# First steps' cached keys gathered and turned, rotation tables and key mask made within layer 0; first half of layer 0's base product as seven block products

## The chip, the cores and the metric

The kernel runs on one core of a Trainium2 chip. Its time is the device time of one execution in microseconds (us); the figure compared is the median of several runs. The engines of the core are named as in the profile: PE (TensorE, matmuls), DVE (VectorE), ACT (ScalarE), POOL (GpSimd), SP (SyncE, which only issues DMAs). Each takes its instructions from a queue of its own, in order.

## What is computed

Four layers follow each other on 8 x 128 tokens of width 512, each of the form x = x + ffn(cond(x)). Two matter here. Layer 0 ends with a mixture of eight low-rank experts over a base product, and layer 2's first part is attention with a paged key and value cache. In the reference's words, cut:

```python
def _L0_ffn_ref(x, base_W, router_W, lora_A, lora_B):
    base = jnp.einsum('bsd,od->bso', x, base_W)
    probs = softmax(einsum('bsd,ed->bse', x, router_W))      # top 2 of 8, renormalised: w_dense
    mid = jnp.einsum('bsd,edr->bser', x, lora_A) * w_dense[..., None]
    return base + jnp.einsum('bser,erd->bsd', mid, lora_B) * 2.0

def _L2_cond_ref(x, Wq, Wk, Wv, Wo, q_norm_w, k_norm_w, k_cache, v_cache, block_table, cache_seqlens):
    q, k, v = projections of x                               # 32 query heads, 8 key heads of 128
    q = _rope(_rmsnorm(q, q_norm_w), pos); k = _rope(_rmsnorm(k, k_norm_w), pos)
    kc = k_cache[block_table]; vc = v_cache[block_table]     # 512 cached tokens of each sequence
    scores = q @ [kc, k] / sqrt(128), -1e30 where the cached key is past cache_seqlens
    return softmax(scores) @ [vc, v] @ Wo.T
```

x here is the output of layer 0's first part, a gated unit with a hidden width of 1376, for the experts, and layer 1's output for the attention.

## The kernel before

All data are fp32; x stays in SBUF as four chunks of 128 features by 1024 tokens. The work is one long program for one core; the tile framework gives buffers and semaphores, and may reorder instructions on an engine unless they are marked (`kept`, in the change also `held`: `keep_in_program_order`). `tc.issue_after(i)` holds instructions back in the order until after i.

**Layer 0, first part.** The hidden units are made in 11 chunks (`gates`, `gates_by_seven`). The second product (`Down`, L598) takes each pair of token quarters (g = 0, 1) and each pair of output chunks (k = 0, 1) by Strassen's scheme: seven block products in place of eight, with sums of weight blocks (`down_weights`, L532, on POOL) and of hidden blocks (`h_sums`, L545, on DVE). `begin`, `go_on` and `out` issue the products, the intermediate reads (L625, L626, L628) and the final sums into `y0` (L640, L642). `transposed(Ad)` uses the buffers tagged `Ad` and `Bg`, which are free afterwards.

**Layer 0, experts** (`experts`, L221). Per half of the tokens: `mids` makes the router logits and low-rank values (L53, copied at L241), `route` the weights (L249 to L277, a chain of small DVE operations with one exponential on ACT), `mix` turns them (L288, L290), and `outs` adds for each of four output chunks the base product, four matmuls of 128x512 over `base0`, and the low-rank product, one matmul, in one bank, and adds the bank to x (L305). The first half's `mids0` and `route0` run among the last `Down` products; `mix0(0)`, `outs0(0)`, and the whole second half follow after the layer's pools have been closed and the attention's pools opened in the same memory. Layer 1 (`adapt`, `mids1`, ..., `outs1`) follows with small products.

**Attention** (`attention`, L807). At its opening DVE makes the mask `hide` (L826 to L834) and POOL the four rotation tables (L844: cosines and sines times the norm weights). The work is 32 steps: 8 key heads x 4 pairs of sequences. Per step n:
- `gather(n, "k")` and `gather(n, "v")`: eight indirect DMAs each, issued by POOL (L928);
- `turn_cached` (L1120): DVE transposes the keys in 32x32 blocks (L1125), SP writes them to DRAM (L1134) and loads them back fully turned into `kT` (L1130);
- `project`: q, k, v by seven products (`seven`, L971; matmuls L985, DVE reads L998, L1000, L1034);
- `squares`, `rotate` (POOL multiplies L1084, DVE L1089), `roots` (for steps 0 and 1 on POOL, L1107 and L1108), `rotated` (L1101), `normed` (L1118): norm and rotation;
- `turn` or, for steps 0 and 1, `turn_at_once` (PE transposes, L1159);
- `weigh`: scores and exponentials (L1179, L1183); `added`, `summed`, `inverted`: the row sums on DVE (L1199, L1209, L1210) and their inverse `R`, by way of DRAM; `mix`: values (L1231); `divided` (L1241); `leave`: output product (L985) with additions to `y2`.

Steps 0 and 1 are woven into the end of layers 0 and 1 by `begin`, `begun` and `first` (L1289 to L1330); `run` (L1332) does the rest. In `first`, `rest()` is called from within step 1's projection; in it POOL clears `y2` (`memset`, L1322). In `run`, POOL then has step 1's rotation (L1084), `roots(1)`, and `gather(2, "k")`; within step 0's part of the loop it has `gather(1, "v")`.

Of the kernel before, what the change touches and what calls it, by code (L numbers as in the profile page):

```python
# [10 lines left out]
F32 = mybir.dt.float32  # L11
I32 = mybir.dt.int32
AF = mybir.ActivationFunctionType
ALU = mybir.AluOpType
# [33 lines left out]
def forward(ctx: ExitStack, tc: tile.TileContext, a: dict, out: bass.AP):  # L48
# [16 lines left out]
    rp = c1.enter_context(tc.tile_pool(name="rp", bufs=1, side="right"))  # L65

    x = xpool.tile([P, DC, NT], F32, tag="x", name="x")

    c0 = ExitStack()
    w0 = c0.enter_context(tc.tile_pool(name="w0", bufs=1))  # L70
# [103 lines left out]


    mask1 = const.tile([P, NB], F32, tag="mask1", name="mask1")
    bias3 = const.tile([P, NB, 8], F32, tag="bias3", name="bias3")
    kvrow = {
        what: const.tile([P, NQ, NB * 4], I32, tag="kvrow_" + what, name="kvrow_" + what) for what in "vk"
# [143 lines left out]
    with c0:  # L323
# [256 lines left out]
        def ranks_to_ranks(wb1T):  # L580
# [2 lines left out]
                mm(ps, wb1T[:, c, :], wmr1[:, c, :], c == 0, c == DC - 1)  # L583
            act.copy(w11, ps)

        tdm = w0.tile([P, NT // 4], F32, tag="tdm", name="tdm")

        def lora_down(AdT):
# [55 lines left out]
        def psp_bank(shape, name):  # L644
            return psp.tile(shape, F32, tag="mm", name=name)

        HB_ = []
        downs = [Down(0, k) for k in range(2)]

# [8 lines left out]
            lora_down(AT)  # L658

        h_sums(0, ypool.tile([P, 3, NH, NT // 4], F32, tag="y", name="hs_0"), meanwhile)  # L660
        for d in downs:
            d.go_on()
        h_sums(1, st.tile([P, 3, NH, NT // 4], F32, tag="hs", name="hs_1", bufs=1), HB_.append)
        y0 = ypool.tile([P, DC, NT], F32, tag="y", name="y0")
        for d in downs:
            d.out()
# [1 line left out]
        downs = [Down(1, k) for k in range(2)]  # L668
        downs[0].begin()
        downs[0].go_on()  # L670
        mids0, route0, mix0, outs0 = experts("l0", wmr0, "probs", 2.0, None, wB0, base0, y0, add_to_x)[:4]
        mids0(0, psp_bank)
        route0(0)
        downs[1].begin()
        downs[1].go_on()
        for d in downs:
            d.out()

# [3 lines left out]
    with psa:  # L682
        c2 = psa.enter_context(ExitStack())
        ps_ = psa.enter_context(tc.tile_pool(name="psa", bufs=2, space=PSUM, reuse_waits="tile"))
        sums = nc.dram_tensor("sums", (HQ * NB // REP, REP * P), F32, kind="Internal").ap()

        def small_bank(shape, name):
            return ps_.tile(shape, F32, tag="av", name=name)

        def large_bank(shape, name):  # L690
            return ps_.tile(shape, F32, tag="st", name=name, bufs=3)


        att = attention(tc, a, x, ident, lens, kvrow, part, ww, wop, ypool, sums, rot, eps, ps_, c2, chunks, mm)

        l1 = att.scratch([P, DC * P + NT], "l1")
        wa1 = l1[:, 0 : DC * P].rearrange("p (c r) -> p c r", c=DC)
        sp.dma_start(wa1, chunks(a["wa1"]))
        t1 = l1[:, DC * P : DC * P + NT]

        def adapt(g):
            tok = slice(g * 512, (g + 1) * 512)
            ps = small_bank([P, 512], f"t1_{g}")
            for c in range(DC):
                mm(ps, wa1[:, c, :], x[:, c, tok], c == 0, c == DC - 1)
            return block_masked(t1[:, tok], ps, mask1, g)

        mids1, route1, mix1, outs1 = experts(
            "l1", None, None, 16.0, br.unsqueeze(1).to_broadcast([P, NB, 8]), wB1, None, None, add_to_x,
            mid_of=lambda tok: [(t1[:, tok], w11)],  # L710
        )[:4]

        mix0(0, large_bank)
        outs0(0, (0, 1), large_bank)
        mids0(1, small_bank)
        route0(1)
        outs0(0, (2, 3), large_bank)
        mix0(1, small_bank)
        outs0(1, (0, 1), large_bank)
        adapted = adapt(0)  # L720
        outs0(1, (2, 3), large_bank)
        mids1(0, small_bank)
        route1(0)
        att.begin()
        att.begun(adapted)
        adapt(1)
        mix1(0, small_bank)
        outs1(0, range(DC), large_bank)
        mids1(1, small_bank)
        route1(1)  # L730
        att.first(lambda: mix1(1, small_bank), lambda *o: outs1(1, o, large_bank))
        kept = nc.dram_tensor("kept_x", (P, DC, NT), F32, kind="Internal").ap()
        c1.close()
        cl = ExitStack()
        late = cl.enter_context(tc.tile_pool(name="late", bufs=1, side="right"))

        def bank(tag, shape, name):
            return ps_.tile(shape, F32, tag=tag, name=name, bufs=2 if tag == "av" else 3)

        def room(tag, shape, name):  # L740

            return (ypool if tag == "y" else wop).tile(shape, F32, tag=tag, name=name)

        def end_of(in_order):
            return ending(
                tc, a, out, x, ident, bias3, experts, late,
                lambda shape, name: ww.tile(shape, F32, tag="q7", name=name),
                lambda shape, name: ww.tile(shape, F32, tag="qs", name=name), room, chunks, mm, in_order,
            )

        y2, end = att.run(late, end_of, bank, lambda: sp.dma_start(kept, x))
        c2.close()
        c3 = ExitStack()
        w3 = c3.enter_context(tc.tile_pool(name="w3", bufs=1, reuse_waits="tile"))
        ex["sm"] = c3.enter_context(tc.tile_pool(name="sm3", bufs=2, side="right", reuse_waits="tile"))
        end.open3(w3, ex["sm"])
        end.layer2(y2, bank, do=range(NB - 2, NB))
# [46 lines left out]
            end.layer3(bank)  # L804


def attention(tc, a, x, ident, lens, kvrow, part, ww, wop, ypool, sums, rot, eps, psa, c2, chunks, mm):  # L807

# [7 lines left out]
    NP = NB // 2  # L818

    ap = c2.enter_context(tc.tile_pool(name="ap", bufs=1))  # L820
    trig, straight, crossed = rot


    kpos = ap.tile([P, 4], F32, tag="kpos", name="kpos")
    for c in range(4):
        dve.tensor_scalar(kpos[:, c : c + 1], part, float(c * P), None, ALU.add)  # L826
    hide = ap.tile([P, NB, 4], F32, tag="hide", name="hide")
    dve.tensor_tensor(
        hide,
        kpos.unsqueeze(1).to_broadcast([P, NB, 4]),  # L830
        lens.unsqueeze(2).to_broadcast([P, NB, 4]),
        ALU.is_ge,
    )
    dve.tensor_scalar(hide, hide, NEG, None, ALU.mult)  # L834


    tabs = {}
    for m in ("k", "q"):
        ws = ap.tile([P, NB, HD], F32, tag="ts" + m, name="ts" + m)
        wx = ap.tile([P, NB, HD], F32, tag="tx" + m, name="tx" + m)  # L840
        for dst, w, tr in ((ws, straight[m], "cos"), (wx, crossed[m], "sin")):
            for i in range(2):
                h = slice(i * 64, (i + 1) * 64)
                pool.tensor_tensor(  # L844
                    dst[:, :, h], w[:, h].unsqueeze(1).to_broadcast([P, NB, 64]), trig[tr], ALU.mult
                )
        tabs[m] = (ws, wx)


    half = ap.tile([P, 2, REP + 1], F32, tag="half", name="half")  # L850
    pool.memset(half, -0.5)
# [1 line left out]
    for k in range(4):  # L853
# [7 lines left out]

    steps = [(qd, p) for qd in range(NQ) for p in range(NP)]
    S = {n: {} for n in range(len(steps))}
    turned, turned_new = (
        nc.dram_tensor("turned_" + name, (len(steps), 4, 32, 4, m, 32), F32, kind="Internal").ap()
        for name, m in (("cached", 8), ("new", 2 * REP + 2))
    )
    W, WO = {}, {}


# [43 lines left out]
    def every(ops):  # L914
        for _ in ops:
            pass
# [203 lines left out]
    def turn_cached(n):  # L1120

        s = S[n]
        t = wk.tile([P, 4, 8, 32], F32, tag="kt", name=f"kt_{n}", bufs=1)
        for j in range(2):
            kept(dve.transpose(  # L1125
                t[:, :, 4 * j : 4 * j + 4, :], s["kc"][j].rearrange("p c (b d) -> p b c d", b=4)
            ))
        s["kT"] = wk.tile([P, 4, 8, 32], F32, tag="kT", name=f"kT_{n}")
        written(turned[n], t)
        return lambda: kept(sp.dma_start(s["kT"], turned[n].rearrange("b i a m d -> (b i) a m d")))  # L1130

    def written(dst, t, by=(sp,)):
# [148 lines left out]

    Y = []

    def scratch(shape, name):
        return wk.tile(shape, F32, tag="pT", name=name)

    late = []

    def begin():  # L1289
        weights(0)  # L1290
        out_weights(0)
        gather(0, "k")
        gather(0, "v")
        every(W[0].factors())

    def begun(behind):

        with tc.issue_after(behind.ins):
            turn_cached(0)()
        gather(1, "k")  # L1300

    def first(mixed, outs_):

# [1 line left out]
        running.append(True)  # L1305
        later = tokens(1, "pT")
        project(0, {
            "u2": lambda: turn_cached(1)(),
            "c22": lambda: every(later),
            "c11": lambda: (squares(0, "k", 0, (0,)), squares(0, "q", 0, (0, 1))),  # L1310
            "c12": lambda: squares(0, "q", 0, (2, 3)),
# [4 lines left out]
        def rest():  # L1316
            squares(0, "q", 1, range(REP))
            squares(0, "k", 1, (0,))
            roots(0)
            y2 = ypool.tile([P, NB, D], F32, tag="y", name="y2")  # L1320
            Y.append(y2)
            kept(pool.memset(y2, 0.0))  # L1322
            keys_terms()
            outs_(0)
            outs_(1)
            rotated(0)
            normed(0)
            outs_(2, 3)
# [3 lines left out]
    def run(pool_, end_of, bank, keep):  # L1332
# [16 lines left out]
        for n, (qd, p) in enumerate(steps):  # L1349
# [40 lines left out]
            summed(n, 0)  # L1390
            if n == 0:
                next(sums_of)
                gather(1, "v")
            every(sums_of)
            if n == 0:
                turn_at_once(1)
# [943 lines left out]
```

## Time and profile before

| | |
|---|---|
| median of 3 runs | 1488.01 us (1486.08 to 1489.38) |
| the profiled execution | 1486.79 us, of it the profiled span 1485.0 us |
| busy: PE, DVE, ACT, POOL | 1471.3, 1063.7, 563.6, 856.4 us |
| TensorE's granted clock | 0.999 |
| PE waits between 210 and 280 us | none listed |
| attention's steps 0 and 1 begin | near 291 us (first `q_one`) |

The profile comes from one execution. It lists every instruction with its start and duration, and for an engine's idle time what released it, inferred from the semaphores. A timeline row reads: start in us from the span's start, us of the group, engine, line and operation, output and inputs by tile name, shapes, how many instructions; in brackets the idle time before it and its releaser. fp32 matmuls show as two records each. "issue" stands for idle time in which the engine waited for nothing that the profile shows.

### The profile page before, as it was taken

The numbers are of one execution on the slowest core, as the hardware profiler recorded it, in microseconds if no ns is written. First come the engines' busy times: TensorE is split into PE (matmuls) and PEld (weight loads), VectorE is DVE, ScalarE is ACT, GpSimd is POOL, SyncE is SP. The second block draws the span as 40 slices with busy tenths as digits, with TensorE's granted clock in tenths as the row PEclk, the third lists the DMA queues.
The fourth block names the chain that finished last, engine by engine and source line by source line (L and its number), as shares of the span: only waits on it lengthen the run. The fifth ranks groups of instructions, "written<-read, shape, count | busy, mean of one in ns | idle before, by whom it ended". The sixth has DMA issues, their size and how long they took to land.

```text
span 1485.0 us, 18055 instructions
## 1 busy us (share of the span) xinstructions
PE 1471.3 (99%) x5571; PEld 934.6 (63%) x5571; DVE 1063.7 (72%) x2121; ACT 563.6 (38%) x1426; POOL 856.4 (58%) x876
## 2 busy tenths in 40 slices
PE   9999999999999999999999999999999999999998
PEld 7888786455556555555655555555555555558886
DVE  4665425478878787787888778787878878855475
ACT  1111110044445544444554454554445455431110
POOL 2241105477767777776777777777777777622310
PEclk9999999999999999999999999999999999999999
DMA  7411001214555544453454455345445534433001
GB/s 242 121 44 32 23 1 62 88 41 126 183 158 148 153 131 128 150 181 117 135 157 129 128 167 172 107 135 164 129 124 165 170 107 137 120 107 98 1 8 52
DMA packets 155993, 172.29 MB, mean 116 GB/s; under 512 B 52784, under 2 KB 126256, under 8 KB 155760
## 3 DMA queue, kind: packets, MB, share of 16 engines
q1 hardware_dynamic: 137712, 134.04, 30.6%
q0 software_dynamic: 17056, 36.49, 7.8%
q8 instruction: 47, 0.77, 0.2%
q10 hardware_dynamic: 1120, 0.52, 0.1%
q14 instruction: 58, 0.48, 0.1%
HBM read 129.95 MB, written 40.76 MB: 115 GB/s over the span
## 4 chain that ended last, share of the span: by engine, by line
PE 94%; DVE 3%; DMA 1%; issue 1%; ACT 0%; SPq 0%; DVEq 0%; ACTq 0%
PE st L1179 18%; PE av L1231 17%; PE g L367 9%; PE q_six L985 8%; PE q_one L985 6%; PE q_five L985 6%; PE wo_two L985 5%; PE dn L367 5%; PE wo_one L985 4%; PE wo_six L985 3%; PE eo_l L53 3%; PE h L1767 2%; PE z L1767 2%; PE o L1767 1%; PE midp_l L53 1%; PE gu L367 1%
## 5 line engine op out<-in xcount | busy, mean ns | idle before, releaser
L928 POOL DMA_INDIRECT kn<-in_k_cache,kvrow_k x256 | 272.1, 1063 | 77.2 <-issue 70.3
L928 POOL DMA_INDIRECT vals<-in_v_cache,kvrow_v x256 | 271.4, 1060 | 73.6 <-issue 59.6
L1231 PE MATMUL av<-pT,vals 128*128 128x512 f32 x640 | 290.8, 592 | 0.2 <-DVE oT L1241 0.2
L1183 ACT ACTIVATE pT<-st,hide 128x512 f32<-128x512 f32 x256 | 175.9, 687 | 191.9 <-PE st L1179 164.3
L1179 PE MATMUL st<-qT,kT 128*128 128x512 f32 x512 | 236.2, 594 | 0.3
L1231 PEld LDWEIGHTS av<-pT,vals 128*128 128x128 f32 x640 | 121.4, 190 | 152.7 <-issue 149.5
L1084 POOL TENSOR_TENSOR vq<-q,txq 128x256 f32<-128x256 f32 x128 | 121.1, 976 | 132.9 <-ACT sqq L1058 93.4
L1179 PEld LDWEIGHTS st<-qT,kT 128*128 128x128 f32 x512 | 96.3, 190 | 110.2 <-issue 105.0
L1199 DVE TENSOR_TENSOR part<-pT 128x512 f32<-128x512 f32 x128 | 88.3, 691 | 77.6 <-ACT pT L1183 64.5
L985 PE MATMUL q_one<-q,x 128*128 128x384 f32 x256 | 93.0, 486 | 0.0
L1058 ACT ACTIVATE sqq<-q 128x128 f32<-128x128 f32 x252 | 78.2, 310 | 10.6 <-DVE q L1034 4.0
L985 PEld LDWEIGHTS q_one<-q,x 128*128 128x128 f32 x256 | 48.5, 190 | 39.8 <-issue 14.1
L985 PE MATMUL q_six<-q_s,xs_all 128*128 128x384 f32 x192 | 69.8, 486 | 0.0
L1039 ACT COPY q<-q_one 128x256 f32<-128x256 f32 x32 | 11.9, 372 | 151.8 <-PE q_one L985 133.5
L985 PE MATMUL wo_one<-o,oT 128*128 128x256 f32 x256 | 65.8, 379 | 0.7 <-DVE oT L1241 0.7
L1179 PE MATMUL st<-qT,kTn 128*128 128x512 f32 x128 | 65.4, 592 | 0.0
L985 PE MATMUL wo_two<-o_s,os 128*128 128x256 f32 x256 | 60.6, 380 | 0.3 <-DVE os L944 0.3
L1183 ACT ACTIVATE pT<-st,rs 128x512 f32<-128x512 f32 x64 | 44.0, 687 | 38.6 <-PE av L1231 13.4
L985 PEld LDWEIGHTS wo_one<-o,oT 128*128 128x128 f32 x256 | 48.6, 190 | 14.2 <-DVE oT L1241 0.8
L436 POOL TENSOR_TENSOR ws<-wu 128x256 f32<-128x256 f32 (+1 forms) x9 | 6.4, 712 | 86.5 <-DMA wu<-in_WuT 86.5
L1215 ACT COPY rows<-rows 32x32 f32<-32x32 f32 x96 | 20.7, 216 | 93.0 <-DVE rows L1210 89.7
L367 PE MATMUL g<-xs,ws 128*128 128x256 f32 (+1 forms) x240 | 55.1, 379 | 0.0
(466 smaller groups left out, 2832.5 us busy)
## 6 DMA issues: line engine op xcount, KB each, us to landing
turned_new<-qkt SPq DMA_DIRECT2D x120, 160.0 KB
turned_cached<-kt SPq DMA_DIRECT2D x128, 128.0 KB
kT<-turned_cached SPq DMA_DIRECT2D x32, 512.0 KB
R<-sums SPq DMA_DIRECT2D x32, 512.0 KB
qT<-turned_new SPq DMA_DIRECT2D x30, 512.0 KB
q<-in_WqT SPq DMA_DIRECT2D x8, 1024.0 KB
o<-in_WoT SPq DMA_DIRECT2D x8, 1024.0 KB
kn<-in_k_cache,kvrow_k POOLq DMA_INDIRECT x256
```

The source lines that it names most:

```text
L53: pe.matmul(o, lhsT, rhs, start=start, stop=stop)
L367: pe.matmul(o, lhsT, rhs, start=start, stop=stop, skip_group_check=True)
L928: kept(pool.indirect_dma_start(out=d[:, c, :], out_offset=None, in_=kc if what == "k" else vc, in_offset=bass.IndirectOffsetOnAxis(ap=kvro ...
L985: kept(pe.matmul(o, l[:, c, :], r[:, c, :], start=start and c == 0, stop=c == 1, skip_group_check=True))
L1058: kept(act.activation(sq, S[n][m][:, j, i, :], AF.Square, accum_out=S[n]["ssq"][:, j, col : col + 1]))
L1084: kept(pool.tensor_tensor(to, t[:, b, :, hi : hi + 64], wx[:, b, lo : lo + 64].unsqueeze(2).to_broadcast(list(to.shape)), ALU.mult,))
L1179: kept(pe.matmul(ps, s["kT"][:, c, 4 * j : 4 * j + 4, :] if c < 4 else s["kn"][:, j], s["qT"][:, :, REP * j : REP * (j + 1), :].rearrange( ...
L1183: kept(act.activation(pT[:, c, :, :].rearrange("p i t -> p (i t)"), ps, AF.Exp, **(dict(bias=hide[:, b, c : c + 1]) if c < 4 else dict(bia ...
L1199: kept(dve.tensor_tensor(o, l, r, ALU.add))
L1215: kept(act.copy(rows[0:32, g, :], rows[32 * g : 32 * g + 32, 0, :]))
L1231: kept(pe.matmul(ps, v[:, c, :], pT[:, c, :, :].rearrange("p i t -> p (i t)"), start=c == 0, stop=c == NC - 1, skip_group_check=True,))
L1767: return pe.matmul(o, lhsT, rhs, start=start, stop=stop, skip_group_check=True)
```

## The change

It has five parts.
1. Within layer 0, behind POOL's weight sums, POOL gathers the cached keys of step 0, later of step 1 (buffer `Ad`), DVE transposes them (buffer `Bg`), and SP writes them to DRAM. In the attention `turn_cached(0)` and `turn_cached(1)` are gone; `cached(0)` and `cached(1)` only load `kT`.
2. The four rotation tables are made by DVE instead of POOL, between the first `Down` of the second half and `route0(0)`, and written to DRAM; the attention loads them (four DMAs of 512 KB on SP).
3. The mask `hide` is made in layer 0, ahead of the last `Down`'s `out()`.
4. The base product of the first token half is taken by seven block products (`Based`), for two pairs of output chunks: 28 matmuls of 128x256 in place of 16 of 128x512; the low-rank product becomes 8 of 128x256 in place of 4 of 128x512. `base_sums` (DVE, in layer 0) and `block_sums` (DVE, after the pools have changed) make the sums. Each k has three intermediate DVE reads and seven DVE additions to x.
5. Gathers move: `gather(0, "v")` waits for layer 1's first adapter product, the sums of step 0's projection weights wait for `finished`, and `gather(1, "v")` stands in `rest()`, right after the `memset` of `y2`, instead of in step 0's part of the loop.

On the engines the order in the compiled program is as written: POOL has `memset(y2)`, eight `vals` gathers of step 1, then step 1's rotation, `roots(1)`, `gather(2, "k")`. PE has step 1's transposes (`turned_1`) at the same place as before, ahead of the last five value products of step 0. DVE interleaves the second half's routing with the block products' reads.

```diff
+        def gather_keys(n):
+            first_keys[n] = t = w0.tile([P, 2, 4, HD], F32, tag="Ad", name=f"kn_{n}")
+            for i in range(8):
+                kept(pool.indirect_dma_start(out=t[:, i // 4, i % 4, :], ...
+        def turn_keys(n):
+            t = w0.tile([P, 4, 8, 32], F32, tag="Bg", name=f"kt_{n}")
+            for j in range(2):
+                kept(dve.transpose(t[:, :, 4 * j : 4 * j + 4, :], ...
+            for q in range(4):
+                kept(sp.dma_start(turned_cached[n][:, :, q]..., t[32 * q : 32 * q + 32]))
+        def rotation_tables():
+            for m, of in enumerate("kq"):
+                for i, (w, tr) in enumerate(((straight[of], "cos"), (crossed[of], "sin"))):
+                    t = w0.tile([P, NB, HD], F32, tag=("Ad", "Bg")[i], name=f"table_{of}{i}")
+                    for l in range(2):
+                        kept(dve.tensor_tensor(t[:, :, h_], w[:, h_]..., trig[tr], ALU.mult))
+                    kept(sp.dma_start(tables_kept[m, i], t.rearrange("p b d -> p (b d)")))
+                yield
...
-        for d in downs:
-            d.go_on()
+        gather_keys(0)
+        downs[0].go_on()
+        turn_keys(0)
+        gather_keys(1)
+        downs[1].go_on()
         h_sums(1, ...)
+        turn_keys(1)
...
         downs[0].begin()
         downs[0].go_on()
+        tabling = rotation_tables()
+        next(tabling)
+        next(tabling)
...
         downs[1].go_on()
+        A0 = base_sums()
+        hidden()
         for d in downs:
             d.out()
...
+            def go_on(self):
+                self.into(odd[:, 1], s1, t1, True)
+                self.into(odd[:, 0], s2, t2)
+                held(dve.tensor_tensor(u, odd[:, 0], p1, ALU.add))
+                held(dve.tensor_tensor(p1, odd[:, 1], p1, ALU.add))
+                self.into(even[:, 1], s3, t3)
+                held(dve.tensor_tensor(p1, even[:, 1], p1, ALU.add))
+                self.into(odd[:, 1], s4, b22)
+                self.into(even[:, 0], a12, b21)
+                self.into(even[:, 1], a22, t4)
...
+        based = [Based(0, k).begin() for k in range(2)]
+        block_sums(0, [yt0[:, n] for n in range(4)])
         mix0(0, large_bank)
-        outs0(0, (0, 1), large_bank)
         mids0(1, small_bank)
+        for b in based:
+            b.go_on()
+            finished = b.finish()
         route0(1)
-        outs0(0, (2, 3), large_bank)
         mix0(1, small_bank)
...
     def begin():
         weights(0)
         out_weights(0)
-        gather(0, "k")
-        gather(0, "v")
-        every(W[0].factors())
+        tabled()
-    def begun(behind):
+    def begun(behind, done):
         with tc.issue_after(behind.ins):
-            turn_cached(0)()
-        gather(1, "k")
+            gather(0, "v")
+        with tc.issue_after(done.ins):
+            every(W[0].factors())
+        for n in range(2):
+            cached(n)()
...
         project(0, {
-            "u2": lambda: turn_cached(1)(),
...
             kept(pool.memset(y2, 0.0))
+            gather(1, "v")
             keys_terms()
...
             if n == 0:
                 next(sums_of)
-                gather(1, "v")
```

## The prediction

> **What bounds the kernel now.** I read the page first, busy time and chain, then who TensorE waited for, then the timelines of the engines from 165 us to 350 us, where all edits lie.
>
> ```profile
> PE 1471.3 (99%) x5571; PEld 934.6 (63%) x5571; DVE 1063.7 (72%) x2121; ACT 563.6 (38%) x1426; POOL 856.4 (58%) x876
> ...
> PE 94%; DVE 3%; DMA 1%; issue 1%; ACT 0%; SPq 0%; DVEq 0%; ACTq 0%
> ```
>
> TensorE is busy 99% of the span and makes up 94% of the chain; its granted clock is 0.999. So only two things change the time: matmul passes taken from TensorE, and stalls put into it or taken out. The list of TensorE's waits between 210 and 420 us is short:
>
> ```profile
> PE q_six L985 <- issue: 1.6, 1, 1.6
> PE midp_l L53 <- DVE l L309: 0.8, 1, 0.8
> ```
>
> No earlier stall stands there that earlier keys, tables or mask could remove. The price of a matmul comes from the chain in order of time (start, us, what; each fp32 matmul shows as two records):
>
> ```profile
> 251.06 8.58 PE eo_l L53 x20
> ...
> 347.96 0.86 PE wo_one L985 x4
> ```
>
> Ten 128x512 matmuls take 8.58 us, 0.86 each; two 128x256 take 0.86, 0.43 each. Half the width costs half, and a product can be cut without loss.
>
> **The block product.** Removed: 16 base matmuls of 512 columns, 16 x 0.86 = 13.75 us. Added: 2 x 7 x 2 = 28 of 256 columns, 28 x 0.43 = 12.03. The low-rank part stays even (4 x 0.86 against 8 x 0.43). TensorE gains **1.7 us**, no more.
> Against it stand VectorE's answers. Each block product needs two reads of one bank (0.42 us each, row of the `du_dn`/`dp_dn` adds) before TensorE may add to that bank again. In layer 0's own block product five matmuls, 2.15 us, cover them. In the new class only two (0.86 us), or four for the first half, because the order list puts the second half's first product between them. I follow the two queues from 238.16 us: first products, four transposes, 16 router matmuls (3.71 us in the chain) until 244.0; `s1*t1`, `s2*t2` until 245.75; `s3*t3` and the other half's `s1*t1` until 247.47. On VectorE the routing of the second token half (12 operations, 4.6 us before at 252.3) now stands in the same queue, interleaved: its first three 256-wide operations end at 246.7, then `u`, one routing operation, and `p1` at 248.05. TensorE waits 0.6 us there, 0.1 for the next read, 0.15 in the second half. Net gain 1.7 - 0.85 = **0.9 us** (bounds: 1.7 without stalls; a loss of 0.5 if each of the four reads is late by a further 0.35, one operation). The sums before it are covered: `base_sums` (8 x 0.45 = 3.6 us) falls into VectorE's idle 6.3 us from 231.6 to 237.9, the mask (2.0 us before, from 239.04) behind it; `block_sums` (4 x 0.69) ends at 241.9, 2.1 us before TensorE asks for it.
>
> **What moves into layer 0.** VectorE is busy 25.0 of 73 us from 165 to 238, GpSimd 0.1, SyncE's queue is silent from 195 to 238.
> - First keys: 16 gathers on GpSimd. The first 8 follow the weight sums (end 165.1) and end near 175; the transposes (1.29 a step) stand in VectorE behind a read that ends at 178.5. The second 8 end near 190, their transposes stand before the `y` copies of 199.66, which move by 1.3 us; TensorE asks for `y` at 217.6. Their eight 128 KB writes go to an empty SyncE queue. Cost nothing; without the cover, VectorE's reads at 190.7 would be late and TensorE would lose what exceeds 1.3 us.
> - Tables: 8 multiplies of 128x512, 0.69 each by the VectorE rows, from 210.05. Two must wait until an earlier table's write has left the buffer. [...] I take nothing.
> - GpSimd loses the table multiplies (10.7 us from 238.55) and the gathers of 249 to 284; nobody waited for them. SyncE gets four 512 KB table loads and two key loads behind the weights, some 16 us at worst, wanted from 297 on; nothing queued behind them is wanted before 314. Nothing.
>
> **Where a stall goes in.** One move is not into layer 0: the values of step 1, `gather(1, "v")`, leave step 0's attention (334 to 345 us on GpSimd) and now stand directly behind `memset(y2)`, ahead of step 1's rotation. GpSimd's timeline, before:
>
> ```profile
> 307.96 3.50 POOL L1322 MEMSET y<- 128x4096 f32 x1
> 313.80 4.20 POOL L1084 TENSOR_TENSOR vq<-q,txq 128x256 f32<-128x256 f32 x4 [2.34 <-DVE q L1034]
> 317.97 1.04 POOL L1084 TENSOR_TENSOR vk<-k,txk 128x128 f32<-128x128 f32 x2
> 319.32 0.23 POOL L1107 TENSOR_SCALAR rs<-ssq 128x10 f32<-128x10 f32 x1 [0.30 <-DVE ssq L1068]
> 319.63 2.82 POOL L1108 TENSOR_TENSOR rs<-rs,half 128x10 f32<-128x10 f32 x1
> 322.63 2.03 POOL L928 DMA_INDIRECT kn<-in_k_cache,kvrow_k  x1 [0.18 <-issue]
> ```
>
> VectorE waits for this chain, and TensorE for VectorE:
>
> ```profile
> 319.40 1.22 DVE L1101 TENSOR_TENSOR r<-r,vq 128x1024 f32<-128x1024 f32 x1
> ...
> 322.49 1.23 DVE L1118 TENSOR_TENSOR r<-r,rs 128x1024 f32<-128x1024 f32 x1 [1.52 <-POOL rs L1108]
> 323.63 1.29 DVE L1199 TENSOR_TENSOR part<-pT 128x512 f32<-128x512 f32 x2
> ```
>
> ```profile
> 327.19 1.26 PE L1159 MATMUL turned<-ident,r 128*128 128x128 f32 x10
> ...
> 343.31 1.45 PE L985 MATMUL q_five<-q,xs 128*128 128x384 f32 x4
> 346.40 1.56 PE L985 MATMUL q_six<-q_s,x 128*128 128x384 f32 x4 [1.64 <-issue]
> ```
>
> The rotated rows are ready at 323.72, TensorE turns them at 327.19: 3.4 us of slack. The idle time before `vq` is 2.34. The gathers: eight at 334 to 344.7 beside a busy VectorE took 1.32 each with their 0.30 gap, 10.6 us; quiet 1.25 (10.0), worst row 1.47 (11.8). [...] The row decides: with this very mix of VectorE work no gather took over 2.03.
> `vq` then starts 8.2 us late. [...] With the quiet figures `vq` is 2.9 instead of 4.2, the power 2.2 instead of 2.8, in all 2.3 us won back. The rotated rows come **6.0 us late** (5.4 to 9.4). TensorE stands 6.0 - 3.4 = 2.5 us at `turned`.
> That isn't all. Behind those rows VectorE has 8.6 us of row sums of step 0, then `R`, `oT` and the read that frees step 2's bank, without a pause of note (0.51) from 323.6 to 344.2. All comes 5.5 us late, TensorE 2.5: it waits about 2.4 more before the fifth product (343.31). Then VectorE's 1.52 us of idle before the next read, in the shadow of TensorE's 1.64 "issue" gap, is used up by its late work. At `q_six` (346.40) both are late by 6.0 - 0.5 - 1.5 = **4.0 us**, and stay so: TensorE has no idle time afterwards to catch up with. GpSimd is free earlier at 345, which nobody awaits.
>
> **Sum.** Against the profiled execution (1486.79, span 1485.0, 1.8 around it; 0.08% under the median): -0.9 + 4.0 = +3.1, so 1489.9, or **1491.1** on the median of 1488.01. A measurement here tells about 0.2%, 3.0 us, from no change.
>
> **Rivals.**
> *Longer stall* (chance 0.22): the 1.64 us gap on TensorE has no cause in the profile; if it falls elsewhere it isn't used up (+1.6), and with slow gathers the delay is 9.4, not 6.0 (+3.4). Or the block product loses 0.5. Time 1493 to 1498, 1495 by the middle. For it: VectorE is busiest just there; against: VectorE goes idle and lets GpSimd go.
> *Not slower* (0.14): the eight gathers hide. It decides where the delay is 2.9 us or less (2.0 absorbed, 0.9 won): the gathers would have to take 7.5 us, 8 x 0.94, with no 0.30 gap between. Time 1488.0. Against it: the page's groups have the gap ahead of 240 of 256 key gathers.
> *The gain alone* (0.04, under 1485): no stall at all, the gap gone, 1.7 + 1.6 = 3.3 off, 1484.7. It needs the move of the gather to be free.
> *My case* (0.60): 1489.3 to 1493, the middle 1491.1. Somewhat over half of it lies above 1491.0.
>
> **Numbers.** Slower by over 0.2%: all of the longer stall and some 0.37 of my 0.60, 0.59. Within: 0.37. Faster: 0.04. The range 1488.0 to 1496.0 leaves out about a tenth on each side.
>
> **What would show it.** TensorE's waits: a new entry `turned <- DVE r` of 2 to 5 us, `q_five` or `q_six` waiting for VectorE, in sum 4 to 6; GpSimd: `vq` of step 1 behind eight `vals`. `eo_l`'s first half replaced by 28 + 8 matmuls, waits under 1 us in sum. Routing at 222 undisturbed. I am wrong if `turned` doesn't wait, if tables push routing beyond 223.5, or if layer 0's end shows more than 1.5 us of new waits.

## The result, and the profile after

The changed kernel takes **1498.35 us** (median of 6, 1496.18 to 1500.63); the kernel before, beside it, 1486.38 (1485.66 to 1489.38). Ratio 1.0077, 95% interval 1.0064 to 1.0090: slower by 12 us, where 3.1 were predicted and 1496.0 was the upper end. The profiled execution is the fastest of the six: 1496.18, span 1494.4, against 1486.79 and 1485.0 before. Repeated in two other groups of runs, the ratio was 1.0045 (1.0031 to 1.0059) and 1.0081 (1.0068 to 1.0095).

The head of the page after:

```profile
PE 1473.5 (99%) x5603; PEld 943.3 (63%) x5603; DVE 1075.3 (72%) x2157; ACT 564.4 (38%) x1428; POOL 845.8 (57%) x868
```

TensorE has 32 more records (each matmul counts as two). It seems 2.2 us busier than before, though the product has 1.7 us less of passes: a first hint that some of them ran slowly. The list of TensorE's waits (who waited for whom, sum, times, longest), from 230 to 1400 us, has three new entries of 2 us or more:

```profile
PE b L794 <- DVE b0u L809: 4.2, 1, 4.2
PE turned L1295 <- DVE r L1249: 3.3, 1, 3.3
PE midp_l L53 <- issue: 2.0, 1, 2.0
```

The first lies inside the new block product (`b`, reads into `b0u`), the second at step 1's rotated rows, the third more than 1100 us behind the change, at layer 3's router. The predicted waits were 0.85, 2.5 and none.

**Half clock.** The busy table by stage (stretch, length, busy us and instructions of PE, PEld, DVE, ACT, POOL, then TensorE's granted clock, DMA share, GB/s):

```profile
238.00:252.00 14.00, 9.85 (x63) 8.78 (x61) 6.50 (x16) 2.40 (x7) 7.73 (x9) 1.00 0.90 327
252.00:256.00 4.00, 4.00 (x11) 3.29 (x12) 3.06 (x11) 0.00 (x0) 0.00 (x0) 0.58 0.59 238
330.00:342.00 12.00, 8.67 (x22) 4.67 (x21) 9.03 (x14) 1.44 (x3) 10.12 (x9) 0.72 0.08 26
```

At the end of the first wait and towards the end of the second (334.96) the clock falls. The trace's clock records have 0.5 for 3.41 us from 251.9 and for 6.83 us from 333.8; in the profile before, there was none until the last 5.6 us of it, from 1481.4 on. The timeline after shows what it does to the four records behind the first wait:

```profile
252.00 2.08 PE L794 MATMUL b<-y,base0s 128*128 128x256 f32 x4 [4.15 <-DVE b0u L809]
```

In a run below that has neither wait nor half clock (e15) the same four take 1.13. From the 0.5 of the records, an estimate: a stretch costs half its length of matmul work, 1.7 us of the 3.41 here, and 2.9 of the 5.7 us that lie behind the second wait. Whether that time is also lost in the end depends on what TensorE would have waited for otherwise; the experiments show both cases. The prediction's sum had no such term.

**Layer 0's end.** ScalarE, VectorE and TensorE in the timeline after:

```profile
244.23 3.62 PE L794 MATMUL b<-yt,base0s 128*128 128x256 f32 x16
...
247.97 0.39 ACT L245 COPY mid_l<-midp_l 128x272 f32<-128x272 f32 x1 [5.00 <-PE b L794]
...
248.39 0.18 DVE L256 TENSOR_REDUCE mx_l<-mid_l 128x4 f32<-128x32 f32 x1 [6.33 <-ACT mid_l L245]
...
250.86 0.42 DVE L808 TENSOR_TENSOR b0u<-b,b0u 128x256 f32<-128x256 f32 x1 [0.55 <-remote]
...
251.53 0.42 DVE L809 TENSOR_TENSOR b0u<-b,b0u 128x256 f32<-128x256 f32 x1
```

The router product that the copy reads ended at 244.40; the prediction had routing begin at once. The copy starts 3.6 us later, routing behind it, and the reads that TensorE needs stand behind routing in VectorE's queue. The trace's semaphore records say where the time goes: TensorE's counts for matmuls that ended at 244.40, 246.12 and 246.99 arrive at 247.95, 250.83 and 250.89. Elsewhere they arrive within 0.02 us (median). TensorE signals late here. The readers show it too, and more firmly, since only 1103 of TensorE's 1388 counts have a record: ScalarE's copy starts at 247.97, and VectorE, free at 250.31, starts the read of `b` at 250.86.

**The attention.** GpSimd, VectorE and TensorE after:

```profile
312.24 3.52 POOL L1458 MEMSET y<- 128x4096 f32 x1
...
325.41 0.94 POOL L1059 DMA_INDIRECT vals<-in_v_cache,kvrow_v  x1 [0.30 <-issue]
326.37 2.77 POOL L1215 TENSOR_TENSOR vq<-q,txq 128x256 f32<-128x256 f32 x4
...
331.56 1.99 POOL L1239 TENSOR_TENSOR rs<-rs,half 128x10 f32<-128x10 f32 x1
333.59 1.22 DVE L1249 TENSOR_TENSOR r<-r,rs 128x1024 f32<-128x1024 f32 x1 [2.18 <-POOL rs L1239]
...
334.96 1.30 PE L1295 MATMUL turned<-ident,r 128*128 128x128 f32 x5 [3.33 <-DVE r L1249]
```

This is the predicted chain: eight gathers, `vq` behind them, `vq` (2.77 where it took 4.20) and the power (1.99 for 2.82) near the prediction's 2.9 and 2.2, the wait at `turned`.

**What was predicted to cost nothing.** The tables' last multiplies and routing after:

```profile
214.24 1.29 DVE L632 TENSOR_TENSOR table_q<-ws_q,cos 128x512 f32<-128x512 f32 x2 [1.59 <-DMA rotation_tables<-table_k]
...
216.17 1.29 DVE L632 TENSOR_TENSOR table_q<-wx_q,sin 128x512 f32<-128x512 f32 x2 [0.64 <-DMA rotation_tables<-table_k]
...
222.14 0.19 DVE L256 TENSOR_REDUCE mx_l<-mid_l 128x4 f32<-128x32 f32 x1 [4.68 <-ACT mid_l L245]
```

The tables end at 217.5, routing begins at 222.14, 0.2 us later than before (221.95). A table's write of 512 KB took some 2.8 us, from its issue at 211.47 to the multiply it lets go at 214.24.

### The profile page after: what moved, and what is told of

Read it like the earlier page. It is cut to its first block, busy times and chain, and to the rows that moved or that the text cites. A ratio compares the mean times of both kernels' runs of the same rounds, so it can differ in the third digit from the quotient of the medians.

```text
span 1494.4 us, 18179 instructions
## 1 busy us (share of the span) xinstructions
PE 1473.5 (99%) x5603; PEld 943.3 (63%) x5603; DVE 1075.3 (72%) x2157; ACT 564.4 (38%) x1428; POOL 845.8 (57%) x868
## 4 chain that ended last, share of the span: by engine, by line
PE 93%; DVE 4%; issue 1%; POOL 1%; ACT 0%; DMA 0%; another core or an unknown queue 0%; DVEq 0%; POOLq 0%; SPq 0%; ACTq 0%
PE st L1315 17%; PE av L1367 17%; PE g L371 9%; PE q_six L1116 8%; PE wo_two L1116 5%; PE q_one L1116 5%; PE q_five L1116 5%; PE dn L371 5%; PE wo_six L1116 4%; PE wo_one L1116 4%; PE h L1903 2%; PE z L1903 2%; PE eo_l L53 2%; PE midp_l L53 1%; PE o L1903 1%; PE gu L371 1%
## 5 line engine op out<-in xcount | busy, mean ns | idle before, releaser
L1059 POOL DMA_INDIRECT kn<-in_k_cache,kvrow_k x240 | 255.1, 1063 | 68.6 <-issue 65.1
```

The costliest lines, as they stand in the source:

```text
L1059: kept(pool.indirect_dma_start(out=d[:, c, :], out_offset=None, in_=kc if what == "k" else vc, in_offset=bass.IndirectOffsetOnAxis(ap=kvro ...
```

## The experiments

Sixteen runs in four groups. Those of a group share a chip; groups 1 and 3 ran on one, groups 2 and 4 on one each. Times therefore stand as ratios to the kernel before in the same group. For stages, the starts of two pairs of TensorE's groups are used, which don't depend on what lies elsewhere: "layer 0's end" from the product's first matmul (with whole products from the four transposes just ahead, which the block product has inside) to the adapter's `t`, and "the attention" from the first `q_one` to the first `wo_one`.

### Group 1: which part

**e1, step 1's values back in the loop.**

```
             kept(pool.memset(y2, 0.0))
-            gather(1, "v")
...
                 next(sums_of)
+                gather(1, "v")
```

> The values of step 1 are gathered again inside step 0's attention, as in the kernel before; all else is as changed. Theory (the gather ahead of step 1's rotation makes TensorE wait 3.3 us at the turned rows, and the wait then costs another 3.4 us because TensorE runs 6.8 us at half clock): the wait and the half clock behind it are gone, the 1.6 us gap before q_six of the kernel before comes back, so about 5 us off the 1498.4: 1493.4. The prediction's own sum had this at 4.0: 1494.4. Rival (the delay of the attention comes from what layer 0 hands on late, not from the gather): within 1 us of 1498.4, with the wait still there.

1.0028 (1.0017 to 1.0040), a fall of 0.5% from the first comparison, where 5 us would be 0.34%. The wait at `turned` is gone, the one at layer 0's end (4.1) stays, with 3.4 us of half clock behind it. The rival falls.

**e2, step 0's values behind the block product.**

```
+        gate = ap.tile([P, 1], F32, tag="gate", name="gate")
+        kept(pool.tensor_copy(gate, x[:, 3, 256:257]))
         with tc.issue_after(behind.ins):
             gather(0, "v")
```

> As changed, but the eight gathers of step 0's values wait (GpSimd reads one element of x that the block product writes last), so they leave the stretch from 239 to 249 us in which the loads run. Theory A (TensorE's completion signals come 3.6 to 4.7 us late there because gathers and loads meet): the 4.2 us wait inside the block product and the 3.4 us of half clock are gone, 4.6 us off: 1493.8, with the second copy of mid at about 244.7 in place of 247.97. Theory B (the loads alone do it): wait and time as they are, 1498.4. Theory C (the chain of waits that TensorE itself carries ahead of the product, for the release of layer 0's buffers): also 1498.4.

1.0056 (1.0034 to 1.0079). The same rows as above, in this run's timeline:

```profile
244.61 3.62 PE L794 MATMUL b<-yt,base0s 128*128 128x256 f32 x16
244.81 0.39 ACT L245 COPY mid_l<-midp_l 128x272 f32<-128x272 f32 x1 [1.47 <-PE midp_l L53]
245.23 0.18 DVE L256 TENSOR_REDUCE mx_l<-mid_l 128x4 f32<-128x32 f32 x1 [2.82 <-ACT mid_l L245]
247.07 0.42 DVE L808 TENSOR_TENSOR b0u<-b,b0u 128x256 f32<-128x256 f32 x1
247.74 0.42 DVE L809 TENSOR_TENSOR b0u<-b,b0u 128x256 f32<-128x256 f32 x1
```

The copy comes 0.2 us behind the start of `b`, no wait is listed inside the product (4.2 as changed), the half clock there is gone, and layer 0's end takes 29.1 us (34.9 as changed, 30.3 before). The loads are all still there, so they alone don't do it (theory B falls), and TensorE's chain of waits stands unchanged (theory C falls).

This run also separates half clock from waiting in the attention. Its wait at `turned` has no half clock behind it, and TensorE waits again instead:

```profile
PE turned L1295 <- DVE r L1249: 3.3, 1, 3.3
PE st L1315 <- ACT pT L1319: 2.0, 1, 2.0
PE q_six L1116 <- DVE vals L1165: 0.4, 1, 0.4
```

The attention takes 62.0 us, as in e16 below with 3.4 us of half clock, and no less than the 61.5 as changed with 6.8. What is late on the other engines sets the end; half clock only fills the time in which TensorE would have waited for it.

**e3, the tables' and keys' loads later.**

```
         out_weights(0)
-        tabled()
...
+        gate = nc.dram_tensor("gate", (P, 1), F32, kind="Internal").ap()
+        tc.keep_in_program_order(sp.dma_start(gate, x[:, 3, 256:257]))
...
+        tabled()
         for n in range(2):
             cached(n)()
...
```

> As changed, but the four table loads and the two loads of turned keys (together 3 MB) wait on SyncE until the block product is done; the weights' loads and the gathers of the values stay where they are. Theory A (gathers and loads meet): wait gone or much shorter, 1494 to 1496. Theory B (loads alone): wait and half clock gone, 1493.8. Theory C (TensorE's own chain of waits): 1498.4, wait of 4.2 us as before. A late table would show as VectorE waiting at about 305 us.

1.0082 (1.0056 to 1.0108). The table by stage:

```profile
248.00:256.00 8.00, 3.87 (x12) 2.83 (x11) 5.57 (x19) 0.23 (x1) 1.97 (x2) 0.82 0.09 25
```

The DMA share fell to 0.09 there, and TensorE is idle as long as before: the wait is 4.1, and the copy of `mid` starts at 247.58 (247.97 as changed). So the loads of tables and keys aren't needed for it. But from 238 to 248 us, the stretch in which the matmuls end whose counts come late, the share is still 0.66 (218 GB/s): the loads of the projection weights, which e3 leaves, among them. By itself e3 doesn't tell whether gathers must meet loads (theory A).

An earlier place tells. From 165 us on, GpSimd now gathers the first keys, and SyncE issues nothing from 163.5 to 180. VectorE's read of `td`, a small product of layer 0, before and after:

```profile
171.52 0.42 DVE L374 TENSOR_TENSOR tdm<-td,half 128x256 f32<-128x256 f32 x1 [1.34 <-PE td L367]
```

```profile
173.82 0.42 DVE L378 TENSOR_TENSOR tdm<-td,half 128x256 f32<-128x256 f32 x1 [3.86 <-remote]
```

The product ended at 171.40 and 171.19. After, the idle VectorE starts its read 2.6 us later, at a DMA share of 0.13 from 171 to 174 us. So beside gathers a count can come late without such loads. Nothing on TensorE waits for this read soon enough to lose by it.

**e4, whole products.**

```
-        A0 = base_sums()
...
-        based = [Based(0, k).begin() for k in range(2)]
-        block_sums(0, [yt0[:, n] for n in range(4)])
         mix0(0, large_bank)
+        outs0(0, (0, 1), large_bank)
         mids0(1, small_bank)
-        for b in based:
-            b.go_on()
-            finished = b.finish()
         route0(1)
+        outs0(0, (2, 3), large_bank)
...
```

> As changed, but the first half of the experts' base product is again 16 whole matmuls; gathers, loads, keys, tables and mask stay. If the 4.6 us of layer 0's end come from the product's waits on VectorE: 1493.8, no wait of TensorE before 300 us, though ScalarE's copy of mid may still come late at 248. If late signals stop TensorE here too: near 1498.

1.0018 (1.0007 to 1.0030), a larger fall than expected: the wait at layer 3's router is gone as well (group 3 says why). One copy of `mid` still comes 1.2 us late, but TensorE waits nowhere for more than 0.3 us from 230 to 300 us. The whole products ask VectorE for nothing in between: a late signal is covered there and bare in the block product.

### Group 2: the parts taken away together

**e5** is e1 and e2 in one; **e6** is e1 and e4; **e7** is e2 with `gather(1, "v")` directly behind `gather(0, "v")`; **e8** is the changed kernel.

> As changed, with both gathers of values moved: step 1's back inside step 0's attention, step 0's behind the block product. The block product, the keys, the tables and the mask stay as changed. Theory (the whole loss comes from where these sixteen gathers stand): no wait above 0.5 us at layer 0's end and none at the turned rows, no half clock there; the block product keeps its 1.7 us less 0.4 of waits, so 1.3 us under the kernel before, ratio 0.9991. Rival (the block product or the moved loads cost by themselves): ratio 1.002 or more.

> As changed, with whole products in layer 0's end and the values of step 1 back inside step 0's attention: what is left of the change is the keys, the tables and the mask in layer 0 (and step 0's values gathered ahead of the product). By the prediction these cost nothing: ratio 1.000 to the kernel before, within 0.1%. Rival (their transfers disturb TensorE or a later queue): 1.002 to 1.004.

> As changed, with the values of steps 0 and 1 both gathered behind the block product, in GpSimd's idle time from 258 to 300 us: no gather of values is left in step 0's attention. If gathers hold back TensorE's signals, the gap of 1.6 us before q_six, which the kernel before has right behind its gathers of step 1's values, is gone as well as the waits: 1.3 + 1.6 = 2.9 us under the kernel before, ratio 0.9980. Rival (sixteen gathers beside layer 1's short products hold signals that TensorE waits for there): new waits of 1 to 3 us between 258 and 285 us, ratio 0.999 to 1.001.

> The changed kernel once more, beside the others on the same chip: ratio 1.0077 as measured first, the 4.2 us wait at layer 0's end and the 3.3 us wait at the turned rows again. If half clock depends on where a wait falls and not on the wait alone, its stretches of 3.4 us come in other places or number than in the first profile.

e5: 1.0010 (1.0003 to 1.0018); e6: 0.9986 (0.9978 to 0.9994); e7: 1.0016 (1.0007 to 1.0026); e8: 1.0045 (1.0031 to 1.0059). e5 and e7 miss: TensorE waits nowhere at layer 0's end or at `turned`, and yet they are slower than before. And e8, the same program, has no late signal in this group, although its gathers stand where they stood; no wait is listed inside its product, and its layer 0's end takes 29.1 us. So at layer 0's end the gathers of the values bring the late signals, but not always: four of the five groups (the first comparison among them) show some, group 2 none. What else it takes stays open. Two things set group 2 apart: its chip, and that its traces hold a record for every one of TensorE's counts, where the others lack about a fifth (1103 of 1388 are there after). Since all timed executions were traced, no run tells whether signals also come late in an execution that isn't.

What e5, e7 and e8 have in common, and e6 has not, is the third new wait, 2.0 us at layer 3's router. The waits in the program say what the profile calls "issue": in the kernels with the block product, this product waits for VectorE's read of `h_6`, the seventh low-rank product of layer 2, a tile it doesn't use. The trace fits: of VectorE's last four reads of `h` after, the third ends at 1395.63, and the product starts at 1395.73. By the program, both tiles lie in PSUM bank 0. In the kernel before, the group `st` is first used and takes banks 0 to 2; the new class uses `mm` first, so that `mm`, in which `h_6` lies, takes bank 0.

### Group 3: the bank

**e9** swaps the two names; no instruction moves on any engine. **e10** is e5, **e11** e7 with the swap; **e12** is the kernel before.

```
-                    ps_.tile([P, 2, NT // 4], F32, tag="st" if k else "mm", name=f"b0_{g}_{k}_{n}", bufs=3)
+                    ps_.tile([P, 2, NT // 4], F32, tag="mm" if k else "st", name=f"b0_{g}_{k}_{n}", bufs=3)
```

> As changed, but the two halves of the block product swap the names of their PSUM banks, so that the bank group first used is the one that was first used before; no instruction moves. The changed kernel has a new wait of 2.0 us far behind the change, at layer 3's first router product (1393.7 us), because that product's bank is now the one that the seventh low-rank product of layer 2 still holds. Theory: with the swap the wait is gone and nothing else, 2.0 us less than the changed kernel (ratio 1.0064 where it has 1.0077, 1.0031 where it has 1.0045). Rival (the wait has to do with instruction fetch or with the place in TensorE's instruction stream): wait and time unchanged, since the stream is the same.

The row after, and then that of e9:

```profile
1395.73 5.65 PE L53 MATMUL midp_l<-wmr,x 128*128 128x200 f32 x32 [2.00 <-issue]
```

```profile
1395.53 5.68 PE L53 MATMUL midp_l<-wmr,x 128*128 128x200 f32 x32
```

The wait is gone, with the stream as it was: the bank, not the fetch of instructions. Ratio 1.0053 (1.0038 to 1.0069), with the 4.2 and the 3.3 us waits still there.

> As changed, with step 1's values back inside the attention, step 0's values behind the block product, and the banks swapped. With all three sources of loss gone what is left is the block product's gain of 1.3 us and whatever the keys, tables and mask gained (2.1 us in the run with those alone): between 0.9975 and 0.999. If the block product by itself costs: above 1.000.

> As changed, with the values of steps 0 and 1 both behind the block product, and the banks swapped. Theory: as the run before, or 1.6 us better if the gap before q_six of the kernel before is due to the gathers of step 1's values: 0.9965 to 0.998. Rival: the early gathers cost at layer 1's end what they save: 0.9985 to 1.000.

> The kernel before itself, for a profile on the chip of these runs. Ratio 1.000. If TensorE's late signals belong to the chip and not to the program, its 1.6 us gap before q_six and the 0.8 us wait at layer 1's router product are there only if the others of this call show late signals beside their gathers too.

e10: 0.9999 (0.9987 to 1.0011), no new wait of TensorE, but above the expected 0.999 (its profile has 3.4 us of half clock far behind the change, see below); e11: 1.0003 (0.9990 to 1.0016); e12: 1.0004 (0.9991 to 1.0017). Late signals are back in this group: e9 waits 4.2 us inside the product again. e11 pays for the early gathers with a new wait:

```profile
PE t L53 <- ACT mid_l L245: 1.4, 1, 1.4
```

So its rival holds. In e12 the 1.6 us gap before `q_six` of the first profile is not there: this gap, too, comes and goes. The attention takes 55.2 us in e12 against 56.7 in the first profile.

### Group 4: a ladder on one chip

**e13** is the changed kernel, **e16** has e2's edit and the swap, **e15** also e1's, **e14** is e15 without the block product.

> The changed kernel as the top of a ladder on one chip. Where TensorE's signals come late beside gathers: ratio 1.0077, with the 4.2 us wait at layer 0's end; where they don't: 1.0045, without it. The 2.0 us wait at layer 3's router and the 3.3 us wait at the turned rows in both cases.

> As changed, with step 0's values behind the block product and the banks swapped, so that of the three sources only the gather ahead of step 1's rotation is left. By the prediction 4.0 us over the run with nothing left; by the theory with half clock 3.3 of wait, up to 2.4 more by the later waits, and 0, 1.7 or 3.4 us for stretches of half clock: 4 to 7 us over it, and 2 us (late signals absent) or 6 to 8 us (present) under the changed kernel.

> As changed with both gathers moved and the banks swapped, the foot of the ladder: 0.9999 was measured on another chip. Theory: 1.3 us (0.0009) under the run without the product on this chip.

> Both gathers of values moved as in the run with both, and whole products in place of the block product: only the keys, the tables and the mask are left of the change. Theory (the block product gains 1.7 us of passes less 0.4 of waits): 1.3 us slower than the run beside it that has the product and swapped banks, so between 0.9985 and 1.0008. Rival (the product costs): faster than that run.

| kernel | what is left | ratio to before (95%) | layer 0's end, us | attention, us |
|---|---|---|---|---|
| e13 | all | 1.0081 (1.0068 to 1.0095) | 35.8 | 61.5 |
| e16 | gather ahead of step 1's rotation | 1.0036 (1.0021 to 1.0051) | 29.1 | 62.0 |
| e15 | none of the three losses | 0.9992 (0.9982 to 1.0001) | 29.1 | 55.3 |
| e14 | nor the block product | 1.0009 (1.0000 to 1.0018) | 30.3 | 54.9 |

From e13 to e16, 0.45% or 6.7 us: layer 0's end and the bank. By the rows these are 6.7 and 2.0; the two intervals leave room for that. From e16 to e15, 0.44% or 6.5 us: the gather (6.6 by the rows). From e14 to e15 the product gains 1.2 us by the rows and 0.17%, 2.5 us, by the times, whose intervals just overlap; e14's profile has 3.4 us of half clock at layer 3, e15's none, which may be part of it. The same stretch of the table by stage, e16 and then e15:

```profile
329.00:342.00 13.00, 12.52 (x33) 6.30 (x34) 11.29 (x22) 5.22 (x11) 8.59 (x8) 0.87 0.14 41
```

```profile
329.00:342.00 13.00, 13.00 (x37) 6.73 (x36) 11.73 (x23) 4.57 (x9) 9.95 (x11) 1.00 0.28 90
```

With nearly the same busy time TensorE gets four records fewer done at a mean clock of 0.87. Of e16's 6.6 us, 3.3 are the wait at `turned`, 1.7 (an estimate, half of it) the 3.4 us of half clock, and the rest small waits (0.3 at `st`, 0.4 at `q_six`, 0.3 at `q_five`) and what the rows don't divide further. In e2 the same 6.6 are 3.3 at `turned`, 2.0 at `st` and the rest, without half clock.

None of the sixteen beats the kernel before by the 0.2% of the prediction's own margin; e6 is the nearest, with 0.14% and an interval below 1, and e15 has 0.08%.

## Why the prediction was wrong, step by step

- **The block product's passes: right.** A gain of 1.7 us less 0.85 of waits, 0.9 in all; where signals come in time (e8, e15, e2) layer 0's end is 1.2 us shorter.
- **Its waits, "0.6 + 0.1 + 0.15": the step that failed.** It followed VectorE's queue from the moment at which routing begins, and took this moment as the end of the router product. In the first comparison the signal came 3.6 us later, and TensorE waited 4.2 us in place of 0.85. The thin cover (0.86 us of matmuls ahead of the first read) was in the prediction, with a loss of 0.5 as its bound; the bound took late reads, one operation each, and no late signal. With half clock behind it, it cost +4.6 us there (30.3 to 34.9) in place of -0.9. Where signals come in time, this step is right: which of the two happens was not to be foreseen from the queues.
- **A bank: the second step that failed.** The prediction put everything behind the attention at nothing. The product at layer 3's router waits 2.0 us (e9 removes it). The names of the PSUM groups were in the kernel, and the waits of the changed program could be read without a run.
- **Half clock: a missing term at layer 0's end.** The prediction counted a wait at its own length. Where nothing else is late, half clock comes on top: layer 0's end takes 34.8 to 35.0 us with 3.4 us of it (after, e1, e3), 35.8 and 36.2 with 6.8 (e13, e9). In the attention it doesn't: 61.5 to 62.0 us, with none (e2), 3.4 (e9, e13, e16) or 6.8 (after, e4, e8); e3, at 63.1, has a further wait of 1.1 ahead of it. The stretches last 3.4 us or twice that; no run shows what sets this length. The profiles have half clock behind waits of 0.5 us, and none behind one of 3.3 (one execution each):

| wait | half clock behind it, us |
|---|---|
| inside the product, 4.1 to 4.2 us | 3.4 (after, e1, e3), 6.8 (e9, e13) |
| at `turned`, 3.3 to 3.4 us | none (e2), 3.4 (e3, e9, e13, e16), 6.8 (after, e4, e8) |
| at layer 3's router, 2.0 us | none (after, e3, e7, e8), 3.4 (e1, e2, e5, e13) |
| among short matmuls, before `hd` of layer 3, 0.4 to 0.8 us | none (before, after, e9, e12, e13, e15, e16), 3.4 (e1, e4, e10, e11, e14), 6.8 (e2, e3) |
| elsewhere, 1.1 to 2.0 us (before, e2, e3, e11) | none |

The waits before `hd` in e2; before, the eight records of `st` behind the same gap took 3.68:

```profile
1314.18 1.04 PE L53 MATMUL hd<-WH,y2T 128*128 128x16 f32 x4 [0.46 <-issue]
1315.06 6.58 PE L1315 MATMUL st<-qT,kT 128*128 128x512 f32 x8
```

So the length of a wait alone doesn't tell whether half clock follows; what does was not settled. Executions of one kernel differ with the clock: in group 4, the 9 of 25 of the kernel before with a mean clock of 0.997 or 0.998 take 1488.3 us on average, the 16 with 0.999 or 1.000 take 1485.6.

- **The gather ahead of the rotation: right in its mechanism, mis-sized by 0.8.** `vq` 8.2 us late against TensorE: 8.3 measured (313.80 to 326.37, less the 4.3 that layer 0 handed on). Rows 6.0 late: 6.8 (323.72 to 334.81, less 4.3). The eight gathers took 10.4 us (predicted 10.0 to 10.6), none of them over 1.57. Of the 2.3 us counted as won back, the trace before shows `vq`'s 2.9 (128 rows, median 0.73, times four) and no row of 2.2 for the power (2.05 and 2.82); that both would run so here was the author's estimate, and after they took 2.77 and 1.99. The 0.8 is `vk`: it takes 1.84 us where it took 1.04, beside VectorE's addition of `vq` (1.46 for 1.22), which the late `vq` had moved there. VectorE now waits 2.18 for the roots where it waited 1.52, and 0.34 for `vk`. `turned` 2.5: 3.3. The prediction's sum, 6.0 - 0.5 - 1.5 = 4.0, gives 4.8 with 6.8 in place of 6.0, and the attention is 4.8 us longer in the first comparison. Against kernels without the gap before `q_six` it is 6.3 (e8 against e5) to 6.6 (e16 against e15): the rival "longer stall" had added 1.6 for that case. The later waits that the prediction put at 2.4 are there in e2 (2.0 at `st`, 0.4, 0.3); elsewhere half clock stands in their place.
- **"The 1.64 gap is used up by late work": not a fixed quantity.** It is gone after, but also in e12 and in e14, where nothing used it up. The prediction treated a stall without a cause in the page as a property of the kernel; it is one of the execution. Its own lines held a sign: VectorE's read of `q_six` at 345.73, with 1.52 us of idle before it, belongs to a product that ended at 342.19, and TensorE goes on at 346.40, when the bank's two reads are done. That fits a late signal beside the gathers of step 1's values, in the kernel before.
- **Keys, tables, mask: nothing.** Right. e14, with these alone, is at 1.0009 and e6, nearly the same, at 0.9986; no row of either shows TensorE waiting for any of them. For the tables no trace before shows a write of 512 KB; the run after has 2.8 us for one and routing 0.2 late. The six loads, given 16 us at worst, took some 13 there, from 241.63 to about 255.
- **Rivals.** "Longer stall" (0.22) was nearest, with 1495 for 1498.35, but by another way: it counted slow gathers and the gap, not late signals. Of the three signs of error named, the third came true: more than 1.5 us of new waits at layer 0's end.

The two profiled executions are 9.4 us apart. By the rows: 0.2 ahead of layer 0's end, +4.6 in it, -0.5 between it and the attention, +4.8 in the attention, and +0.3 behind it, in which the bank's 2.0 is made good by other differences. The medians are 12.0 apart, mostly because the profiled execution after is the fastest of its six; the other 2.6 are not divided here.

## What to carry over

Ask of every new stall what else is late at that place. Where nothing is, half clock behind the stall is lost on top (1.7 us and more at layer 0's end); where the next work is late anyway, the lateness of that work sets the cost, and half clock only fills it. A product that asks another engine for an answer in the middle needs cover for a late signal, not only for the work in the queue: here 0.86 us stood against counts 3.6 to 4.7 us late. An "issue" gap beside gathers in the profile before, like the 1.64 us at `q_six`, can be a sign of such signals. And when a new tile is the first user of a PSUM group, look at which later tiles change banks: here the wait, 2.0 us, appeared more than 1100 us behind the change.

## What was not expected of the hardware

While GpSimd issued gathers, TensorE's counts arrived late: 3.6, 4.7 and 3.9 us after the matmul's end at layer 0's end after, the last two in a bunch (250.83 and 250.89), some 1.7 us after the last gather's end (249.15). Without the gathers there they came in time (e2: the copy at 244.81, no wait inside the product); with the loads of tables and keys put later they didn't (e3: a wait of 4.1 us), and `td` was read 2.6 us late beside gathers at a DMA share of 0.13. One group of runs showed none of it at layer 0's end with the same gathers (e8: 29.1 us, no wait inside the product). By what path gathers and late counts hang together, and why not always, was not settled.
